# Turning the attention's mixed values on VectorE in 32x32 squares instead of on TensorE

## The chip, the core and the metric

The kernel runs on one core of one Trainium2 chip. The metric is the time of one launch on the device in microseconds (us), as the median of several runs; each run executes the whole kernel once. Besides, one execution is recorded by the hardware profiler, and every duration of a single instruction comes from that one.

The core has five engines that work side by side, each on its own queue, in order. PE is TensorE's matrix multiplication and PEld its loading of weights, DVE is VectorE, ACT is ScalarE, POOL is GpSimd, SP only issues transfers. TensorE writes its results to PSUM, a memory of eight banks of 512 f32 columns on 128 partitions; VectorE and ScalarE fetch them from there into SBUF, the working memory.

## The reference

The input is x of shape (8, 512, 256) in f32: 8 batches of 512 tokens. Four layers follow on each other, each on the normed x and added to x: a scan layer, a mixture of experts, an attention, and the same mixture again.

```
x = x + scan(layernorm(x))          # silu(x Win), decaying state, y Wout
x = x + ffn(layernorm(x))           # 16 routed experts, 4 chosen per token, and a shared one
x = x + attention(layernorm(x))
x = x + ffn(layernorm(x))

# attention, H = 16 heads of DK = 16, T = 512 tokens, per batch
q, k, v = split(x @ Wqkv.T)
scores  = clip(q @ k.T * 0.25, -10, 10) + causal_mask
out     = softmax(scores) @ v       # (H, T, DK) -> (T, 256)
return out @ Wout.T
```

The change is in the attention alone, between the product with v and the product with Wout.

## The kernel before

**Stages.** There are four: the scan, the blocks of the routed experts, the attention, and the routed blocks again. `stretch` runs the scan and, later, the attention over the eight batches. In each of them the norm, the router and the shared expert of the mixture that follows are worked in beside: while batch b has its attention, the shared expert of batch b - 2 and the router of batch b - 1 and b - 2 run, and the norm and the projections to q, k and v of the batches ahead. Batches 0 and 1 have no shared expert beside them.

**What sets the order.** Each piece of work is a generator that yields the number of TensorE columns of its next step. `beside` takes the next step from the piece that is least far on, by share of its columns; `behind` puts pieces one after another; `timed` places steps at given shares of the way. What comes out is a program, and a scheduling layer then sets the order on each engine from the dependences and its own costs, apart from instructions that are kept in program order.

**Buffers.** A pool has a number of buffers per tag, which its tiles take in turn: a new tile waits until the one whose buffer it gets has been read for the last time. In SBUF these are "col" (6 buffers of 512 columns: es of the third bank, oT, sig, the router's larger tiles) and "kb4" (9 buffers of 1024 columns). In PSUM the attention has four single banks ("one": po, pto, pt, pq, pv, pg, pd, py, pl, pr) and two pairs ("pair": the scores ps).

**The attention of one batch** (`Attention.main`, from L1100). The 16 heads are four groups (o, w): o is the half of the 256 columns, w says which of two neighbouring heads, and a group holds four heads, j = 0 to 3, each on 32 partitions. For a group:

- `weights` (L1120, L1131, L1134, L1142): the scores of four heads, transposed (key tokens on the partitions), into ps; ScalarE takes their exponential into es; VectorE clips it, and the causal triangle with it.
- `mix` (L1155): v times the weights into po, 128 partitions x 512 tokens. The stationary operand of a head has 32 columns: its 16 values, a column of ones, and 15 that are not needed. So po has for head j, on partitions 32j to 32j + 15, the mixed values not yet divided; on partition 32j + 16 the sum of the weights, by which they are to be divided; then 15 rows of no use.
- `share` (L1168 to L1174): the division. [...] ScalarE copies po to SBUF (oT, L1168), TensorE turns it in four 128x128 transposes into pto (L1171), where tokens lie on the partitions and the sum of a head is beside its values; VectorE takes the reciprocals (rec, L1173) and multiplies (o, L1174).

When all four groups are done, `turned` (L400, L402; tiles pt_oa and xT_oa) turns o back by eight 128x128 transposes, and ScalarE and VectorE each copy one half to SBUF, since the next product needs the 256 columns on the partitions. Then `add_projection` (L457, L466; tile py_a) multiplies by Wout and adds to x.

`weights` of a group is written before `mix` of the group before it, and `share` after both; in batches 2 to 6 (`close`) the two are one step.

The names that appear below besides: pq_a, pv_a (L1065, L1083) the projections to q, k and v, with L1076 VectorE's part of k; pg_m, pd_m (L982, L1011) the shared expert, with sig_m and act_m on ScalarE and VectorE (L996 to L1002); pt_m, pl_m (L400, L595) the router's transposes and logits, whose turning (L606) is a transpose of VectorE; pick, sel (L657, L665) the router's choice; rstd_l (L435) the norm's power on GpSimd; xg (L723) the scatter of the rows to their experts by GpSimd.

Of the kernel before, what the change touches and what calls it, by code (L numbers as in the profile page):

```python
# [10 lines left out]
FP = mybir.dt.float32  # L11
# [4 lines left out]
P = 128  # L16
SQ = 32
QUAD = P // SQ
B, T, D = 8, 512, 256
NT = T // P  # L20
KD = D // P
# [3 lines left out]
H, DK = 16, 16  # L25
HG = 4
NO = H * DK // P
# [29 lines left out]
KB, COLS = 9, 6  # L57
# [19 lines left out]
def tile_hybrid_block(  # L77
# [22 lines left out]
    nc = tc.nc  # L100
# [3 lines left out]
    work = ctx.enter_context(tc.tile_pool(name="work", bufs=2))  # L104
    small = ctx.enter_context(tc.tile_pool(name="small", bufs=2))
# [3 lines left out]
    def bank(shape, name: str, kind: str = "one"):  # L109
        kind = instead.get(kind, kind)  # L110
        return stage[kind].tile(shape, FP, tag=kind, name=name)
# [54 lines left out]
    ident = const.tile([P, P], FP, name="ident")  # L166
# [119 lines left out]
    steps = const.tile([P, NJ], FP, name="steps")  # L286
# [101 lines left out]
    def turned(src, tag: str, into, copies, home=None, past=None):  # L388

        rows = src()  # L390
        if home is None:
            dst = work.tile([P, KD, T], FP, tag="kb4", name=f"xT_{tag}", bufs=KB)
        else:
            dst = home(f"xT_{tag}")
        into(dst)
        for k in range(KD):
            pt = bank([P, NT, P], f"pt_{tag}_{k}")
            for t in range(NT):
                with tc.issue_after(past[-1].ins) if past else nullcontext():
                    nc.tensor.transpose(pt[:, t, :], rows[:, t, k * P : (k + 1) * P], ident)  # L400
            flat = pt.rearrange("p t q -> p (t q)")
            copies[k](dst[:, k, :], flat)  # L402
            yield T // 2

    by_both = (nc.scalar.copy, nc.vector.tensor_copy)
# [40 lines left out]
    def kb4(name: str):  # L446
        return work.tile([P, NT, D], FP, tag="kb4", name=name, bufs=KB)
# [583 lines left out]
    def spot(kind: str, rows: int):  # L1031
        first, many, n = spots[kind]
        spots[kind][2] = (n + 1) % many
        at = first_expert * WEXP + (first + n) * NT * D
        return w_all[:, at : at + NT * D].rearrange("p (a b) -> p a b", a=rows)

    class Attention:
# [60 lines left out]
        def main(self, b: int, made):  # L1098
            q_sb, k_sb, v_sb = made
            tag = f"a{b}"  # L1100
            held = {}

            def weights(o: int, w: int, i: int, at):


                tiles, cols = BANKS[i]
                ps, es = [], []
                for two in range(2):
                    name = f"{tag}_{o}_{w}_{i}_{two}"
                    ps.append(bank([P, 2, T], f"ps_{name}", "pair"))  # L1110
                    if cols == T:
                        es.append(spot("es", 2))
                    else:
                        es.append(work.tile([P, 2, cols], FP, tag="col", name=f"es_{name}", bufs=COLS))
                col = 0
                for c in tiles:
                    n = T - c * P
                    for j in range(HG):
                        r = slice(32 * j, 32 * j + 32)
                        nc.tensor.matmul(  # L1120
                            ps[j // 2][:, j % 2, col : col + n],
                            lhsT=k_sb[w][r, o, c * P : (c + 1) * P],
                            rhs=q_sb[r, o, c * P : T],
                            start=True,
                            stop=True,
                        )
                        at[c, j] = es[j // 2][:, j % 2, col : col + n]
                    col += n
                mixed = len(tiles) * P
                for two in range(2):  # L1130
                    nc.scalar.activation(es[two], ps[two][:, :, 0:cols], AF.Exp, scale=ATT_SCALE)  # L1131
                    diagonal = es[two][:, :, 0:mixed]
                    limit = causal[:, 0 : len(tiles), :].rearrange("p c q -> p (c q)")
                    nc.vector.scalar_tensor_tensor(  # L1134
                        diagonal,
                        diagonal,
                        LOW,
                        limit.unsqueeze(1).to_broadcast([P, 2, mixed]),
                        ALU.max,
                        ALU.min,  # L1140
                    )
                    nc.vector.tensor_scalar(es[two][:, :, mixed:], es[two][:, :, mixed:], LOW, TOP, ALU.max, ALU.min)  # L1142
                return T + (len(tiles) - 1) * T

            order = [c for tiles, _ in BANKS for c in tiles]

            def mix(o: int, w: int, i: int, at):


                if i == 0:  # L1150
                    at["po"] = bank([P, T], f"po_{tag}_{o}_{w}")
                for c in BANKS[i][0]:
                    for j in range(HG):
                        h = 8 * o + 2 * j + w
                        nc.tensor.matmul(  # L1155
                            at["po"][32 * j : 32 * j + 32, c * P : T],
                            lhsT=v_sb[:, c, h * VC : h * VC + 32],
                            rhs=at[c, j],
                            start=(c == order[0]),
                            stop=(c == order[-1]),  # L1160
                            tile_position=(0, 32 * j),
                        )
                return len(BANKS[i][0]) * T

            def share(o: int, w: int, at):

                oT = work.tile([P, T], FP, tag="col", name=f"oT_{tag}_{o}_{w}", bufs=COLS)
                nc.scalar.copy(oT, at["po"])  # L1168
                pt = bank([P, NT, HG, 32], f"pto_{tag}_{o}_{w}")
                for t in range(NT):  # L1170
                    nc.tensor.transpose(pt[:, t].rearrange("p j c -> p (j c)"), oT[:, t * P : (t + 1) * P], ident)  # L1171
                rec = small.tile([P, NT, HG], FP, tag="rec", name=f"rec_{tag}_{o}_{w}")
                nc.vector.reciprocal(rec, pt[:, :, :, DK])  # L1173
                nc.vector.tensor_mul(  # L1174
                    held["o"].rearrange("p t (o j w c) -> p t o j w c", o=NO, j=HG, w=2)[:, :, o, :, w, :],
                    pt[:, :, :, 0:DK],
                    rec.unsqueeze(3).to_broadcast([P, NT, HG, DK]),
                )

            def steps():  # L1180
                held["o"] = kb4(f"o_{tag}")
                groups = [(o, w, {}) for o in range(NO) for w in range(2)]

                close = 1 < b < B - 1
                last = None
                for o, w, at in groups:
                    for i in range(len(BANKS)):


                        columns = weights(o, w, i, at)  # L1190
                        if last is not None and not close:
                            yield columns
                            columns = 0
                        if last is not None:
                            columns += mix(*last[0:2], i, last[2])
                        yield columns
                    if last is not None:
                        share(*last)
                        yield T // 2
                    last = o, w, at  # L1200
                for i in range(len(BANKS)):
                    yield mix(*last[0:2], i, last[2])
                share(*last)
                yield T // 2
                yield from turned(lambda: held["o"], f"o{tag}", lambda oT: held.update(oT=oT), by_both)
                yield from add_projection(b, lambda c: held["oT"][:, c, :], wo_sb, KD, tag)

            each = 2 * NT * T + T // 2
            return Piece(2 * NO * each + KD * T // 2 + NT * KD * D, steps())


    ready, unturned = {}, {}
# [336 lines left out]
```

## Time and profile before

| what | us |
|---|---|
| median of 3 runs | 1742.05 |
| the runs | 1734.45, 1742.82, 1742.05 |
| the profiled execution | 1735.83 |
| its span, first to last instruction | 1734.1 |
| TensorE busy | 1648.4 (95%) |
| VectorE busy | 1110.7 (64%) |
| ScalarE busy | 788.7 (45%) |
| GpSimd busy | 773.0 (45%) |
| mean TensorE clock granted, share of full | 0.985 |

The attention goes from about 744 us (first projection) to about 1243 us (last product with Wout); from there to 1301 us the shared experts of batches 6 and 7 and the last router follow, then the routed blocks.

A row of a group of instructions reads: line, engine, operation, tiles written and read, shape, count; then the busy time in us and the mean ns of one; then the idle time of the engine just before, and what ended it. A row of the waits reads: who waited, for whom, us in total, times, longest. A row of the timeline reads: start and length in us, engine, line, operation, count. Matrix multiplications in f32 are two passes each in the trace, transposes one; they overlap in TensorE's pipeline, so the length of one is more than the time by which it delays the next.

### The profile page before, as it was taken

The numbers are of one execution on the slowest core, as the hardware profiler recorded it, in microseconds if no ns is written. First come the engines' busy times: TensorE is split into PE (matmuls) and PEld (weight loads), VectorE is DVE, ScalarE is ACT, GpSimd is POOL, SyncE is SP. The second block draws the span as 40 slices with busy tenths as digits, with TensorE's granted clock in tenths as the row PEclk, the third lists the DMA queues.
The fourth block names the chain that finished last, engine by engine and source line by source line (L and its number), as shares of the span: only waits on it lengthen the run. The fifth ranks groups of instructions, "written<-read, shape, count | busy, mean of one in ns | idle before, by whom it ended". The sixth has DMA issues, their size and how long they took to land. (4 is left out here: it accounts for less than half of the span.)

```text
span 1734.1 us, 32869 instructions
## 1 busy us (share of the span) xinstructions
PE 1648.4 (95%) x10640; PEld 1225.8 (71%) x10640; DVE 1110.7 (64%) x3463; ACT 788.7 (45%) x1724; POOL 773.0 (45%) x675
## 2 busy tenths in 40 slices
PE   6899998999999999999999999999998999998993
PEld 3566655589999999944445545544558999998992
DVE  7888877545556655566776676676754755565562
ACT  3223232155555555555544454364315555554551
POOL 3356556435555555530042332332543555555563
PEclk8999999999999999999999999999999999999997
DMA  4454423445555665531011212122544555566666
GB/s 160 147 179 151 148 93 121 153 95 95 96 95 104 105 101 95 106 62 38 25 65 50 77 51 72 55 73 84 192 138 89 96 96 97 111 138 124 122 120 166
DMA packets 149277, 181.37 MB, mean 105 GB/s; under 512 B 16144, under 2 KB 135984, under 8 KB 149104
## 3 DMA queue, kind: packets, MB, share of 16 engines
q0 software_dynamic: 54720, 82.57, 25.6%
q1 hardware_dynamic: 92576, 92.71, 17.9%
q10 hardware_dynamic: 1808, 3.93, 0.6%
q8 instruction: 89, 1.46, 0.4%
q14 instruction: 84, 0.69, 0.1%
HBM read 81.62 MB, written 97.53 MB: 103 GB/s over the span
## 5 line engine op out<-in xcount | busy, mean ns | idle before, releaser
L930 POOL DMA_INDIRECT part<-rows x272 | 425.9, 1566 | 341.5 <-ACT rows L929 236.7
L723 POOL DMA_INDIRECT xg<-sorted_m,slots_m x256 | 258.3, 1009 | 267.6 <-ACT slots_m L720 91.9
L893 PEld LDWEIGHTS ph<-rows,gate 128*128 128x128 f32 x2160 | 282.0, 191 | 16.1 <-ACT rows L883 1.9
L893 PE MATMUL ph<-rows,gate 128*128 128x128 f32 x2160 | 285.5, 275 | 0.6 <-ACT rows L883 0.6
L893 PE MATMUL ph<-rows,up 128*128 128x128 f32 x2160 | 285.3, 275 | 0.0
L921 PE MATMUL pyr<-w_all,rows 128*128 x1088 | 279.8, 380 | 0.4 <-DVE rstd_l L431 0.4
L893 PEld LDWEIGHTS ph<-rows,up 128*128 128x128 f32 x2160 | 262.9, 192 | 0.0
L901 ACT ACTIVATE rows<-ph 128x256 f32<-128x256 f32 x272 | 104.2, 383 | 328.5 <-PE ph L893 328.5
L902 DVE TENSOR_TENSOR rows<-ph,rows 128x256 f32<-128x256 f32 x272 | 115.2, 424 | 190.4 <-ACT rows L901 189.4
L921 PEld LDWEIGHTS pyr<-w_all,rows 128*128 128x128 f32 x1088 | 185.5, 190 | 14.9 <-ACT rows L929 0.8
L875 ACT COPY gate<-w_all 128x512 f32 x270 | 168.8, 626 | 14.2 <-PE ph L893 2.4
L1131 ACT ACTIVATE w_all<-ps_a 128x1024 f32<-128x1024 f32 x128 | 124.4, 1021 | 68.8 <-PE ps_a L1120 63.7
L875 DVE COPY up<-w_all 128x512 f32 x270 | 118.1, 437 | 30.3 <-PE ph L893 17.5
L929 ACT ACTIVATE rows<-pyr,gain 128x256 f32<-128x256 f32 x272 | 128.4, 472 | 14.3 <-PE pyr L921 12.2
L906 DVE SCALAR_TENSOR_TENSOR gain<-rows,expert_b 128x4 f32<-128x4 f32 x272 | 61.2, 225 | 107.9 <-ACT rows L929 82.4
L1120 PE MATMUL ps_a<-w_all 32*128 32x384 f32 (+3 forms) x1024 | 120.0, 468 | 8.0 <-ACT w_all L1131 6.3
L982 PE MATMUL pg_m<-xT_m,su_sb 128*128 128x512 f32 x256 | 123.4, 604 | 0.0
L982 PE MATMUL pg_m<-xT_m,sg_sb 128*128 128x512 f32 x256 | 122.3, 599 | 0.0
L903 DVE TENSOR_TENSOR rows<-ph,rows 128x256 f32<-128x256 f32 x272 | 115.0, 423 | 8.4
L1011 PE MATMUL pd_m<-sd_sb,act_m 128*128 128x256 f32 x512 | 120.0, 382 | 0.0
L1011 PEld LDWEIGHTS pd_m<-sd_sb,act_m 128*128 128x128 f32 x512 | 95.4, 190 | 22.0 <-issue 5.7
L882 PE MATMUL pt<-ident,rows 128*128 128x128 f32 x544 | 103.7, 273 | 6.2 <-DMA rows<-xg 4.8
(228 smaller groups left out, 2176.7 us busy)
## 6 DMA issues: line engine op xcount, KB each, us to landing
rows<-xg SPq DMA_DIRECT2D x272, 136.0 KB, 2.5
part<-x SPq DMA_DIRECT2D x16, 512.0 KB, 2.9
part<-ys_m SPq DMA_DIRECT2D x14, 512.0 KB, 3.1
w_all<-in_L_ffn_gate_w_dram SPq DMA_DIRECT2D x24, 256.0 KB, 5.4
w_all<-in_L_ffn_up_w_dram SPq DMA_DIRECT2D x24, 256.0 KB, 5.4
w_all<-in_L_ffn_down_w_dram SPq DMA_DIRECT2D x24, 256.0 KB, 5.8
sum<-part POOLq DMA_DIRECT2D x10, 512.0 KB, 4.1
xg<-zeros SPq DMA_DIRECT2D x34, 136.0 KB, 1.8
```

What stands on the lines that cost most here:

```text
L723: nc.gpsimd.indirect_dma_start(out=xg[i], out_offset=bass.IndirectOffsetOnAxis(ap=slots[:, at : at + 1], axis=0), in_=rows[:, t, :], in_of ...
L875: copy(here, w_all[:, bass.ds(held[n][0] + half * KD * F, KD * F)])
L893: nc.tensor.matmul(ph[:, s, f * P : (f + 1) * P], lhsT=both[s][:, k * F + f * P : k * F + (f + 1) * P], rhs=rows[:, ROW + k * P : ROW + (k ...
L902: nc.vector.tensor_mul(act, ph[:, 0, :], act)
L903: nc.vector.tensor_mul(act, ph[:, 1, :], act)
L921: nc.tensor.matmul(py, lhsT=act[:, f * P : (f + 1) * P], rhs=w_all[:, bass.ds(w + 2 * KD * F + f * D, D)], start=(f == 0), stop=(f == KF - 1),
L929: nc.scalar.mul(rows[:, 0:D], py, gain[:, TK : TK + 1])
L930: nc.gpsimd.indirect_dma_start(out=parts[i][n % 2], out_offset=bass.IndirectOffsetOnAxis(ap=rows[:, D + 2 * TK : D + 2 * TK + 1].bitcast(U ...
L982: made = nc.tensor.matmul(dst, lhsT=w[:, k, f * P : (f + 1) * P], rhs=xnT[:, k, :], start=(k == 0), stop=(k == KD - 1),)
L1011: nc.tensor.matmul(py[:, j, :], lhsT=acts[n][:, f, t * P : (t + 1) * P], rhs=shared[n][3][:, f, :], start=(n == 0 and f == 0), stop=(n == ...
L1120: nc.tensor.matmul(ps[j // 2][:, j % 2, col : col + n], lhsT=k_sb[w][r, o, c * P : (c + 1) * P], rhs=q_sb[r, o, c * P : T], start=True, st ...
L1131: nc.scalar.activation(es[two], ps[two][:, :, 0:cols], AF.Exp, scale=ATT_SCALE)
```

## The change

Instead of copying po and turning it on TensorE, VectorE's transpose reads po from PSUM and turns each square of 32 x 32 by itself, into the tile tr: square (j, q) of po, head j and tokens 32q to 32q + 31, stays in its place and is turned within it. So on partition 32j + s there is, in square q, token 32q + s of head j: 16 values and, in column 16 (DK), its sum. One reciprocal for each partition and square, and a multiplication, divide. The group w = 0 does so in place, in columns 0 to 15 of each square; the group w = 1 writes its divided values beside them, in columns 16 to 31 of the tile of w = 0 (`both`). A second transpose of VectorE then turns the squares back, into half o of oT; the squares' rows are now 32j + 16w + c, which is the order of the 256 columns of the product with Wout. oT is read there directly.

The copies by ScalarE, the four transposes of each group, the eight of `turned`, and its two copies go; and with them their steps in the generator (the steps of `share` count no columns now, and the piece's total is smaller by as much).

```diff
             def share(o: int, w: int, at):
 
-                oT = work.tile([P, T], FP, tag="col", name=f"oT_{tag}_{o}_{w}", bufs=COLS)
-                nc.scalar.copy(oT, at["po"])
-                pt = bank([P, NT, HG, 32], f"pto_{tag}_{o}_{w}")
-                for t in range(NT):
-                    nc.tensor.transpose(pt[:, t].rearrange("p j c -> p (j c)"), oT[:, t * P : (t + 1) * P], ident)
-                rec = small.tile([P, NT, HG], FP, tag="rec", name=f"rec_{tag}_{o}_{w}")
-                nc.vector.reciprocal(rec, pt[:, :, :, DK])
+                tr = work.tile([P, T // SQ, SQ], FP, tag="col", name=f"tr_{tag}_{o}_{w}", bufs=COLS)
+                nc.vector.transpose(tr.rearrange("p q c -> p (q c)"), at["po"])
+                rec = small.tile([P, T // SQ], FP, tag="rec", name=f"rec_{tag}_{o}_{w}")
+                nc.vector.reciprocal(rec, tr[:, :, DK])
+                both = held.setdefault(o, tr)
                 nc.vector.tensor_mul(
-                    held["o"].rearrange("p t (o j w c) -> p t o j w c", o=NO, j=HG, w=2)[:, :, o, :, w, :],
-                    pt[:, :, :, 0:DK],
-                    rec.unsqueeze(3).to_broadcast([P, NT, HG, DK]),
+                    both[:, :, w * DK : (w + 1) * DK],
+                    tr[:, :, 0:DK],
+                    rec.unsqueeze(2).to_broadcast([P, T // SQ, DK]),
                 )
+                if w == 1:
+                    nc.vector.transpose(held["oT"][:, o, :], both.rearrange("p q c -> p (q c)"))
 
             def steps():
-                held["o"] = kb4(f"o_{tag}")
+                held["oT"] = work.tile([P, NO, T], FP, tag="kb4", name=f"oT_{tag}", bufs=KB)
...
                     if last is not None:
                         share(*last)
-                        yield T // 2
+                        yield 0
...
                 share(*last)
-                yield T // 2
-                yield from turned(lambda: held["o"], f"o{tag}", lambda oT: held.update(oT=oT), by_both)
+                yield 0
                 yield from add_projection(b, lambda c: held["oT"][:, c, :], wo_sb, KD, tag)
 
-            each = 2 * NT * T + T // 2
-            return Piece(2 * NO * each + KD * T // 2 + NT * KD * D, steps())
+            return Piece(2 * NO * 2 * NT * T + NT * KD * D, steps())
```

In the kernel after, the first transpose has line L1168, the reciprocal L1170, the multiplication L1172 and the second transpose L1178; lines after that are lower by two than before.

## The prediction

> **What bounds the kernel now.** I read the busy totals first, then the stretches of the attention stage, its groups of instructions, TensorE's waits, and the timeline of one batch's end.
>
> ```profile
> PE 1648.4 (95%) x10640; PEld 1225.8 (71%) x10640; DVE 1110.7 (64%) x3463; ACT 788.7 (45%) x1724; POOL 773.0 (45%) x675
> ```
> ```profile
> 803.00:851.00 48.00, 46.39 (x362) 22.01 (x361) 38.33 (x125) 27.73 (x40) 3.23 (x4) 1.00 0.11 34
> ...
> 1045.00:1110.00 65.00, 64.23 (x408) 32.03 (x404) 44.79 (x132) 31.99 (x54) 18.25 (x18) 1.00 0.16 55
> ...
> 1175.00:1244.00 69.00, 64.37 (x453) 33.48 (x452) 50.82 (x175) 28.69 (x51) 23.75 (x26) 1.00 0.41 135
> ```
>
> The second fence is busy time by stretch: start:end, length, then PE, PEld, DVE, ACT, POOL. The three rows are about batch 1, a middle batch and batch 7 of the attention. TensorE has nearly no idle time in any; VectorE stands at 38.33/48 = 80%, 69% and 74%. A microsecond of TensorE's queue that goes is therefore a microsecond of the span, unless TensorE then waits. Who makes it wait now (first to last microsecond of the attention proper, 744 to 1244):
>
> ```profile
> PE ps_a L1120 <- ACT w_all L1131: 6.3, 12, 1.0
> PE pto_a L1171 <- DVE w_all L1076: 2.5, 4, 0.8
> PE pto_a L1171 <- ACT oT_a L1168: 1.1, 1, 1.1
> PE pt_oa L400 <- DVE o_a L1174: 1.0, 1, 1.0
> ```
>
> Three of the four lines, 4.6 us, stand before the very transposes that the change deletes. The groups concerned, and the one stream transpose that the kernel already has:
>
> ```profile
> L1171 PE MATMUL pto_a<-ident,oT_a 128*128 128x128 f32 x128 | 19.8, 277 | 3.7 <-DVE w_all L1076 2.5 <-ACT oT_a L1168 1.1
> L400 PE MATMUL pt_oa<-ident,o_a 128*128 128x128 f32 x64 | 9.9, 278 | 1.0 <-DVE o_a L1174 1.0
> L1168 ACT COPY oT_a<-po_a 128x512 f32<-128x512 f32 x32 | 19.0, 592 | 30.4 <-PE po_a L1155 28.0 <-DVE row_m L678 2.4
> L1174 DVE TENSOR_TENSOR o_a<-pto_a,rec_a 128x256 f32<-128x256 f32 x32 | 13.5, 422 | 0.7
> L1173 DVE RECIPROCAL rec_a<-pto_a 128x16 f32<-128x16 f32 x32 | 8.1, 252 | 12.8 <-PE pto_a L1171 12.8
> L402 DVE COPY xT_oa<-pt_oa 128x512 f32<-128x512 f32 x8 | 5.5, 692 | 9.5 <-PE pt_oa L400 9.5
> L606 DVE STREAM_TRANSPOSE logit_m<-pl_m 128x128 f32<-128x128 f32 x16 | 5.0, 312 | 18.0 <-PE pl_m L595 17.9
> ```
>
> The mean of 277 ns is the length of one transpose, not what it costs the queue. That is read from successive starts at the end of batch 0:
>
> ```profile
> 798.91 0.50 PEld L1171 LDWEIGHTS pto_a<-ident,oT_a 128*128 128x128 f32 x4
> ...
> 799.38 0.47 PEld L400 LDWEIGHTS pt_oa<-ident,o_a 128*128 128x128 f32 x4
> ...
> 799.82 0.73 PEld L1083 LDWEIGHTS pv_a<-w_att,xT_l 128*128 128x128 f32 x4
> ```
>
> Four transposes take 0.47 and 0.44 us, on average 0.455.
>
> [...]
>
> **The change, part by part.**
> *Removed from TensorE:* per batch 4 blocks for pto and 2 for pt_oa, of four each; in 8 batches 48 x 0.455 = 21.8 us. With them go the 4.6 us of waits in front: 26.4 us at most.
> *Removed from ScalarE:* per batch 4 x 0.592 + 0.585 (its half of xT_oa) = 2.95 us, 24 us in all. ScalarE is at 45 to 60% in these stretches; the saving counts only where the exponentials (L1131) hold TensorE, the 6.3 us above. I take nothing and keep 6 us for the good end.
> *VectorE.* Removed per batch: 4 x (0.252 + 0.422) + 0.692 = 3.39 us. Added: 4 transposes of 128x512 from PSUM, 2 from SBUF, 4 reciprocals and 4 multiplications, now from SBUF. PSUM rows of 256 and 512 columns (0.422, 0.692) give 1.05 ns per column, so 0.312 + 384 x 1.05 ns = 0.71 us. From SBUF I take 0.70; the lower end is 0.437, which a 128x512 SBUF copy takes (L875), the upper for both 1.25 = four times 0.312. Reciprocal 0.25 and multiplication 0.41 (SBUF rows of that size, L690) as now. Sum 4 x (0.71 + 0.25 + 0.41) + 2 x 0.70 = 6.9 us: 3.5 more per batch, 28 us in all. A middle batch goes from 44.8/65 to 48.3/62 = 78%, batch 1 to some 41.8/45 = 93%. It is beside TensorE, but the queue is in order.
> *The new wait* is at each batch's end. Built, the program puts behind the last mixing matmul one py_a, two pd_m pairs, one py_a, a pd_m, and then the py_a whose weights are the second half of oT. Each is two passes of 0.215 us (16 passes of py_a take 3.81 us with the tail), so that is 7 x 0.43 = 3.0 us of cover. The chain on VectorE: the drain of po 0.3, transpose 0.71, reciprocal 0.25, multiplication 0.41, transpose 0.70, with the router's pick and sum (0.41 + 0.58) queued between: some 3.3 us. The stall is 0.3 us in middle batches, about 0.5 in batches 0, 1 and 7, whose cover is other work. If the scheduler's neighbours are late, 1.5 us. Behind the waiting py_a stand the next batch's scores, and so ScalarE.
> *PSUM.* po's bank is now freed by VectorE (0.71 us, in order behind the clips L1134 and L1142), not by ScalarE. Where VectorE is behind, as in the first group of a middle batch, where pto waited 0.8 us for L1076, the next po or pg waits. 4 + 2 of 34 banks per batch are no longer asked for, which works the other way. I put 0.4 us per batch on it.
> *SBUF.* The "col" tile of w = 0 now lives until the group w = 1 is turned back, one of six gone for a quarter of a batch; a "kb4" tile per batch is saved. Priced under the rivals.
> *POOL:* four xg scatters stand ahead of the power of rstd_l (L435) in batches 2 to 5; they take 1.27 us each from start to start, the xn that waits stands over ten us later, so nothing. No DMA is added; SP's order is the same.
>
> Sum: 26.4 - 8 x (0.4 + 0.4) = 20.0, less 1 for batch 1 at 93%: **19 us saved**; ends 8 and 32.
>
> **The rivals.** *A, as above.*
> *B, it saves more:* fewer PSUM banks and a freer ScalarE also end the 6.3 us of ps_a waits, and py_a never waits: 26.4 + 6 = 32 us. For it: three of four waits sat there. Against: VectorE's queue.
> *C, VectorE's lateness takes back most:* at 1.25 us per transpose its time per batch grows by another 6 x 0.54 = 3.3 us, and chain and bank waits cost 1.5 to 2.5 us per batch: 26.4 - 16 = 10 us or less saved; about nothing at 3 us per batch.
> *D, slower:* the held col tile. ScalarE's exponentials of the third bank (es_a) and sig_m come from the same six buffers; if each of the 32 groups has one that waits for VectorE's turn back, TensorE stops behind it. It decides above 26.4/32 = 0.8 us per group; at 1.2 us it is 12 us slower. Against it: some 22 col tiles per batch, so the sixth after is mostly past the release.
> *E, the saving is not in the span* because the scatters of batch 7 set the end of the stage: they end at 1291.6 us and TensorE's work before the routed blocks at 1301, so 9 us are free. Excluded unless the scatters slip.
>
> **How the numbers follow.** The profiled execution took 1735.8 us (span 1734.1); the runs have 1734.5, 1742.1 and 1742.8, so it is 6 us below their median. Half of the runs lie at either level; I start from 1738. A: 1738 - 19 = **1719** (1708 to 1732), chance 0.62. B: 1706, 0.14. C: 1728 to 1738, 0.17. D: 1750, 0.07. The range, 1703 to 1736, leaves out D and the ends. A measurement of this kernel can tell about 0.5%, some 9 us: faster (below 1733.3) 0.83, same 0.10, slower 0.07.
>
> **What would show it.** Right: no pto or pt_oa rows; TensorE's gaps before py_a under 5 us in all; the two transpose groups near 0.71 and 0.70 us; VectorE 27 us busier, ScalarE 24 less; the attention 20 us shorter, all other stages as they were. Wrong: transposes over 1 us, PE waits on L1168 or L1178 above 10 us, or es_a and sig_m waiting for VectorE.

## The result and the profile after

The kernel after takes 1729.24 us (median of 7 runs, 1726.29 to 1733.52), the kernel before 1738.88 us (7 runs): a ratio of 0.9943, 95% interval 0.9926 to 0.9961. That is faster by about 10 us, where the prediction's sum was 19 us. Two further sets of runs gave 0.9946 [0.9927, 0.9965] and 0.9934 [0.9908, 0.9959]. The profiled execution took 1730.08 us (span 1728.4).

The engines' totals, as the page has them:

```profile
PE 1638.1 (95%) x10448; PEld 1210.7 (70%) x10448; DVE 1131.6 (65%) x3503; ACT 767.9 (44%) x1684; POOL 772.8 (45%) x675
```

192 matrix multiplications are gone, VectorE is 20.9 us busier, ScalarE 20.8 less busy. The groups that the change brings, from the groups of instructions:

```profile
L1168 DVE STREAM_TRANSPOSE tr_a<-po_a 128x512 f32<-128x512 f32 x32 | 22.7, 710 | 24.6 <-PE po_a L1155 24.6
L1178 DVE STREAM_TRANSPOSE oT_a<-tr_a 128x512 f32<-128x512 f32 x16 | 11.2, 697 | 0.3
L1172 DVE TENSOR_TENSOR tr_a<-tr_a,rec_a 128x256 f32<-128x256 f32 x32 | 13.3, 417 | 0.2
L1170 DVE RECIPROCAL rec_a<-tr_a 128x16 f32<-128x16 f32 x32 | 7.8, 245 | 0.0
```

The durations are those of the prediction: 0.710 and 0.697 us for the transposes (0.71 and 0.70 taken). So VectorE's prices are not where the 9 us went. The waits of TensorE in the attention (744 to 1244 us) say more:

```profile
PE ps_a L1120 <- ACT w_all L1131: 6.7, 15, 1.0
PE pt_l L400 <- DVE tr_a L1168: 2.6, 1, 2.6
PE po_a L1155 <- DVE tr_a L1168: 2.0, 4, 0.5
PE pr_m L673 <- DVE sel_m L665: 2.0, 1, 2.0
```

The waits in front of pto and pt_oa are gone. Two single waits have come, of 2.6 us (pt_l, in batch 1) and 2.0 us (pr_m, the router's product, in batch 7), and a small one in four of the middle batches. The timeline shows the two:

```profile
843.79 0.71 DVE L1168 STREAM_TRANSPOSE tr_a<-po_a 128x512 f32<-128x512 f32 x1
844.55 0.66 PE L400 MATMUL pt_l<-ident,xn 128*128 128x128 f32 x4 [2.57 <-DVE tr_a L1168]
1221.08 0.43 PE L673 MATMUL pr_m<-sel_m,tri 128*128 128x64 f32 x2 [1.99 <-DVE sel_m L665]
```

pt_l wants the bank of a po that the transpose at 843.79 has to read first, and that transpose stands on VectorE behind the router's choice (L641 to L654) and two clips. In batch 7 sel stands behind a transpose (L1168, from 1219.33) and more clips; whether that transpose is why TensorE waits is taken up under e4.

The last thing to see is in the busy time by stretch, in the third column from the right, the granted clock of TensorE (start:end, length, then PE, PEld, DVE, ACT, POOL). The first two rows are about batch 1 and a middle batch, the others lie in batch 7:

```profile
803.00:852.00 49.00, 44.17 (x339) 19.51 (x338) 41.08 (x131) 26.07 (x36) 3.23 (x4) 1.00 0.11 33
1045.00:1110.00 65.00, 64.42 (x405) 31.00 (x404) 49.27 (x153) 29.28 (x49) 20.08 (x20) 1.00 0.17 60
...
1184.89:1191.72 6.83, 6.83 (x33) 1.89 (x29) 6.62 (x24) 3.39 (x7) 0.00 (x0) 0.50 0.14 41
1191.72:1222.44 30.72, 27.22 (x230) 10.77 (x228) 25.47 (x86) 14.72 (x25) 16.81 (x16) 1.00 0.50 167
1222.44:1225.85 3.41, 3.41 (x7) 1.17 (x4) 1.72 (x7) 0.93 (x4) 0.00 (x0) 0.50 0.64 178
```

In two stretches, 6.83 and 3.41 us long, the clock is 0.50. The second begins 1.4 us after the wait for sel ends. TensorE counts as fully busy in them (6.83 of 6.83), so neither busy time nor waits show the loss: 7 instructions take the 3.41 us. The profile before had no such stretch in the attention.

Batches, from the last py_a of one to that of the next (starts in the timeline; batch 0 from the first pq_a), in us:

| | 0 | 1 | 2 | 3 | 4 | 5 | 6 | 7 | sum |
|---|---|---|---|---|---|---|---|---|---|
| before | 60.2 | 48.0 | 69.2 | 67.9 | 67.6 | 67.8 | 66.0 | 51.6 | 498.3 |
| after | 58.0 | 49.3 | 65.0 | 65.2 | 65.2 | 65.2 | 63.5 | 55.9 | 487.3 |
| saved | 2.2 | -1.3 | 4.2 | 2.7 | 2.4 | 2.6 | 2.5 | -4.3 | 11.0 |

Six batches gain 2.2 to 4.2 us, where the prediction's terms give 2.5 for one; batches 1 and 7 lose. With the 5.1 us that the two stretches at half clock cost at most (half of 10.24), batch 7 would be 50.8 us.

### The profile page after: what moved, and what is told of

It reads as the page before. It is cut to its first block, busy times and chain, and to the rows that moved or that the text cites. A ratio compares the mean times of both kernels' runs of the same rounds, so it can differ in the third digit from the quotient of the medians.

```text
span 1728.4 us, 32460 instructions
## 1 busy us (share of the span) xinstructions
PE 1638.1 (95%) x10448; PEld 1210.7 (70%) x10448; DVE 1131.6 (65%) x3503; ACT 767.9 (44%) x1684; POOL 772.8 (45%) x675
```

## The experiments

**Two theories.** *1:* the gain in TensorE's queue came through, less two single waits (batches 1 and 7); the rest went to TensorE's clock, which is halved after a wait. *2:* VectorE's lateness, spread over the batches and reached through po's banks, took it; the clock only accompanies it.

Each run lists its granted clock, so the clock's share can be estimated for runs without a profile too: time x (1 - clock), called the clock loss below; what is left of the time is the rest. For the profile of after this gives 37.9 us, which is half of what its stretches at 0.50 last. Two limits go with it. It counts also the stretches of the first 355 us, 12 us of loss in each profile of the two kernels, and the last one, where TensorE has no work: 24 to 25 us long in the two profiles of before, 26 to 28 in the three of after, so about 1 us of a difference between the two may be no loss. And it is an upper estimate: a stretch of 6.83 us in batch 7 of before (under e1) made that batch 1.6 us longer, not 3.4.

The runs in a table (medians; "clock loss" and "rest" are means over the runs; batches from the profile; runs of one kernel in several sets are joined in the first two rows, whose times are means). The runs of before come from three chips, and on each the rest is 1708.6 to 1709.3 us. The means of five to eight runs have standard errors of 0.6 to 1.9 us, so 2 us between two of these kernels are hardly clear of the scatter.

| kernel | us | ratio to before, 95% | clock loss | rest | batches 0, 1, 7 |
|---|---|---|---|---|---|
| before (85 runs) | 1739.3 | 1 | 30.4 | 1708.9 | 60.2, 48.0, 51.6 |
| after (23 runs) | 1728.9 | see above | 35.9 | 1693.0 | 58.0, 49.3, 55.9 |
| e3 old in batch 7 | 1725.1 | 0.9921 [0.9893, 0.9950] | 31.9 | 1692.9 | 59.3, 50.9, 53.2 |
| e4 po by ScalarE | 1727.6 | 0.9938 [0.9915, 0.9961] | 35.8 | 1692.0 | 59.8, 47.7, 55.6 |
| e5 fill | 1727.1 | 0.9933 [0.9908, 0.9958] | 31.1 | 1695.6 | 57.3, 50.8, 58.3 |
| e6 before, fill | 1739.1 | 0.9996 [0.9981, 1.0012] | 26.9 | 1710.8 | 59.5, 48.0, 51.7 |
| e7 sel first | 1725.1 | 0.9912 [0.9882, 0.9942] | 34.1 | 1689.7 | 59.4, 50.9, 53.0 |
| e8 all three | 1723.7 | 0.9908 [0.9881, 0.9936] | 31.0 | 1692.0 | 57.3, 47.7, 56.1 |
| e14 fill for sel | 1727.3 | 0.9924 [0.9899, 0.9949] | 33.5 | 1693.9 | 62.1, 50.8, 55.2 |
| e15 product later | 1723.0 | 0.9897 [0.9864, 0.9929] | 33.0 | 1689.6 | 59.7, 50.8, 53.5 |
| e16 all | 1720.8 | 0.9887 [0.9857, 0.9916] | 30.7 | 1690.2 | 57.3, 47.7, 54.6 |

The batches of before and after are those of the first profiles. The second profile of before has 61.4, 48.0 and 53.2 us, the second and third of after 62.6, 50.9, 55.9 and 58.0, 49.3, 56.0.

**e1 and e2, the two kernels once more, for their clocks.**

> The kernel before, unchanged, for the granted clock of several of its executions. In its one profile 1.7 us are lost between 500 and 1700 us to stretches in which TensorE's clock is halved (one stretch, at 1306.5), in the profile of the kernel after 11.95 us (six, two of them in batch 7). Theory 1, the change makes such stretches more frequent: the clocks of the runs here are 0.983 to 0.986 (those of after were 0.977 to 0.983, mean 0.980), so 5 to 8 us of the missing gain are clock. Theory 2, the stretches fall by luck and VectorE's queue took the gain: the clocks here scatter around 0.980 too, and the profile of this run has some of the stretches between 1000 and 1700.

> The kernel after, unchanged, once more. Theory 1: the halved stretches near 1184.9 and 1222.4 (the end of batch 7) come again in this profile, though the 3.41 us grid on which the clock is set lies elsewhere, since the waits in front of them (1.0 us for the exponential, 2.0 us for the router's sel) are in the program's order: at least one of the two. Theory 2: they need not come again, but batch 7 then stays longer than before's 51.6 all the same. Time 1727 to 1732, ratio 0.993 to 0.996.

Over all sets the clock loss is 30.4 us before (standard error 0.4) and 35.9 us after (0.7): 5.6 us more, 95% about 4.0 to 7.1. The rest is 16.0 us less (14.8 to 17.1). Theory 1 holds in that, though before's clocks were lower than I expected (0.979 to 0.986, mean 0.9826). The second profile of before has a stretch of 6.83 us in batch 7 too, after a wait of 1.0 us for the exponential, and one of 3.41 us in batch 0:

```profile
1202.50:1209.33 6.83, 6.83 (x35) 1.85 (x30) 6.35 (x24) 3.26 (x6) 0.00 (x0) 0.50 0.14 38
```

So these two can come without the change, as theory 2 had it; whether the change makes them more frequent, two profiles of before can't tell. (The expectation speaks of six stretches in after; they are five, at 1184.9, 1222.4, 1294.1, 1543.3 and 1580.8.) The second profile of after has both stretches of batch 7 again, at 1192.2 and 1229.7, and one more behind the wait of pt_l in batch 1:

```profile
847.43:850.84 3.41, 0.83 (x8) 0.42 (x4) 3.31 (x21) 0.00 (x0) 0.00 (x0) 1.00 0.00 0
850.84:854.26 3.42, 3.42 (x21) 1.78 (x20) 1.17 (x3) 0.00 (x0) 0.00 (x0) 0.50 0.01 2
```

In 3.41 us TensorE was busy for 0.83, and the next 3.41 us are at 0.50. In the first profile the same wait lay across the edge of two such windows (1.58 and 0.99 us idle), and no stretch followed.

**e3, batch 7 as before.** `share` of the kernel before for `b == B - 1`.

```diff
+                if b == B - 1:
+                    oT = work.tile([P, T], FP, tag="col", name=f"oT_{tag}_{o}_{w}", bufs=COLS)
+                    nc.scalar.copy(oT, at["po"])
...
+                    return
```

> The kernel after, but batch 7 divides and turns as in the kernel before (ScalarE's copy, TensorE's 24 transposes), which is about 2.7 us more for TensorE. Theory 1: with the transposes back in batch 7, the wait for sel and the halved stretches there go, so batch 7 takes 51.6 instead of 55.9 us and the whole 1724 to 1727 us, a ratio of 0.991 to 0.993, at a mean clock 0.002 to 0.003 higher than after's. Theory 2 (VectorE's lateness is spread over all batches): batch 7 is worth at most 2 us and the ratio stays at 0.993 to 0.996.

With 24 transposes more the kernel is 4.8 us faster than after beside it (means; 95% about 0.6 to 9). The wait for sel is gone, and its stretch; the one after the exponential stays (at 1188.2), so batch 7 has 53.2 us and not 51.6, as in the second profile of before. The clock loss is smaller (31.9 against 35.9), and the rest did not grow by the transposes' 2.7 us, since the 2.0 us of the wait went.

**e4, po's bank freed by ScalarE.**

```diff
+                raw = work.tile([P, T], FP, tag="col", name=f"raw_{tag}_{o}_{w}", bufs=COLS)
+                nc.scalar.copy(raw, at["po"])
-                nc.vector.transpose(tr.rearrange("p q c -> p (q c)"), at["po"])
+                nc.vector.transpose(tr.rearrange("p q c -> p (q c)"), raw)
```

> The kernel after, with po copied to a col tile by ScalarE (0.59 us, as in the kernel before), and VectorE's first transpose reading that tile: po's PSUM bank no longer waits for VectorE's queue, VectorE's work is the same. Theory 2, bank waits: the waits for the transpose (po 2.0 us, pt_l 2.6 us) and of the weights go, 4 to 8 us faster than after, ratio 0.989 to 0.991. Theory 1: the waits go, but they are worth at most their 4.6 us; the time falls by 2 to 5 us, less what 32 more copies on ScalarE delay the exponentials (0 to 4 us): ratio 0.991 to 0.994.

All waits for tr_a are gone. Batch 1 takes 47.7 instead of 49.3 us and has no stretch at half clock, the middle batches 65.0 instead of 65.2. So the bank is the cause in batch 1, and worth 0.2 us in a middle batch, of 0.4 us put on it. The whole is 1.8 us faster than after beside it, give or take 2.9, so not clear of the scatter: the wait for sel grew to 2.8 us.

```profile
1220.93 0.57 DVE L665 TENSOR_REDUCE sel_m<-pick_m 128x64 f32<-128x256 f32 x1
1221.42 0.70 DVE L1170 STREAM_TRANSPOSE tr_a<-raw_a 128x512 f32<-128x512 f32 x1
1221.56 0.43 PE L673 MATMUL pr_m<-sel_m,tri 128*128 128x64 f32 x2 [2.84 <-DVE sel_m L665]
```

Here sel stands in front of the transpose, and TensorE waits longer than in after. Counted from the last py_a of batch 6, sel is done after 43.6 us in e4, 43.7 in after and 43.5 in the second profile of before, each with the same stretch of 6.83 us earlier in the batch. So the change hardly delayed sel. What it changed is TensorE: without its transposes it is ready for the router's product 41.8 us into the batch in after, and 40.8 us in e4, where the product stands eight mixing products earlier in its queue. In before it comes to it at 44.3 us and waits for nothing. TensorE became early; VectorE's transposes did not make sel late.

**e5 and e6, idle transposes in after and in before.**

```diff
+                many = {(0, 1): 4, (0, 2): 8, (B - 1, 2): 8}.get((b, i), 0) if o == w == 0 else 0
+                if many:
+                    spare = bank([P, T], f"spare_{tag}_{i}")
+                    with tc.issue_after(held["ps"].ins):
+                        for n in range(many):
+                            nc.tensor.transpose(spare[:, 0:P], ident, ident)
```

> The kernel after with 20 more transposes of the constant ident by TensorE, whose result nobody reads: 4 and 8 of them stand in front of the scores of the second and third bank in the first group of batch 0, 8 in front of those of the third bank in the first group of batch 7. There TensorE waits for the exponential (0.5, 0.4, 0.9 and 1.0 us) and, in the profiles so far, the clock is halved right after. The 20 cost 2.2 us of TensorE's queue, in the waits' time. Theory 1 (the clock): the stretch of 6.8 us near 1185 is gone and that near 765 too, so the kernel with more work is 3 to 6 us faster than after, 1723 to 1726 us, ratio 0.990 to 0.993, mean clock at least 0.982. Theory 2 (the clock is a symptom, or falls by luck): no change or up to 2 us slower, 1729 to 1731 us, clock 0.978 to 0.980.

> The same 20 transposes in the kernel before. Its second profile has the same stretches near 765 and 1202, its first has not. Theory 1: the clock rises from 0.9825 to 0.984 or more and the time falls by 2 to 4 us, to 1735 to 1737 us; if so, these two stretches are not of the change's making, and what the change adds to the clock's loss are those after its own waits (sel in batch 7, pt_l in batch 1). Theory 2: within 1 us of before.

In batch 0 the stretch is absent in both. The place in after without and with the transposes; first two rows of e2:

```profile
762.10:765.51 3.41, 1.77 (x18) 0.97 (x20) 1.96 (x5) 2.86 (x5) 0.00 (x0) 1.00 0.76 256
765.51:775.75 10.24, 10.24 (x40) 2.60 (x40) 4.76 (x12) 3.96 (x5) 0.00 (x0) 0.50 0.06 19
```

and one row of e5:

```profile
761.90:768.70 6.80, 6.20 (x48) 2.87 (x48) 4.97 (x13) 5.62 (x8) 0.00 (x0) 1.00 0.44 151
```

Batch 0 takes 57.3 us, against 58.0, 62.6 and (e13, below) 58.0 in the three profiles of after. In batch 7 they do fill the wait that they were meant for: 0.2 us are left of 1.0, and no stretch follows. But the batch got longer (58.3 us), since TensorE then waits 2.1 us for a later exponential. That one stands on ScalarE behind slots_m, which waits for VectorE:

```profile
1185.61 0.70 PE L1126 MATMUL ps_a<-w_all 32*128 32x256 f32 x4 [0.21 <-ACT w_all L1137]
1190.42 0.29 ACT L720 CAST slots_m<-choices_wm 128x2 uint32<-128x2 f32 x2 [1.40 <-DVE choices_wm L696]
1191.68 1.14 PE L1126 MATMUL ps_a<-w_all 32*128 32x128 f32 x12 [2.08 <-ACT w_all L1137]
```

In after TensorE runs through that place at half clock and does not wait there. In e5 a stretch of 3.41 us follows this wait, and one of 6.83 us the wait for sel. As a whole e5 gained 1 to 2 us and e6 nothing: the clock loss fell (by 4.8 and by 2.7 to 3.5 us), and the rest grew by about the 2.2 us of the transposes. More TensorE work for no time, then, but not the 3 to 6 us that I expected.

**e7, sel earlier on VectorE; e8, all three together.** In e7 pick and sel get a higher priority in the scheduling layer, and the transpose of the third group is queued behind sel:

```diff
+                late = b == B - 1 and summed.get((1, B - 2))
+                with tc.issue_after(late.ins) if late else nullcontext():
+                    nc.vector.transpose(tr.rearrange("p q c -> p (q c)"), at["po"])
```

> The kernel after, but in batch 7 the router's pick and sum (sel) are put ahead of two clips and of the transpose of the third group on VectorE's queue, some 1.25 us earlier. The wait of the router's product for sel is 2.0 us in after. Theory 1: it becomes 0.7 us, [...] so the stretch of 3.4 us near 1222 (1.7 us lost) goes as well: 3 us faster than after, 1726 us, ratio 0.992 to 0.993. Theory 2, only the wait itself counts, and VectorE's work behind it is as late as before: at most 1.3 us, ratio 0.994.

> The kernel after with the three together: po copied by ScalarE, sel first in batch 7, the 20 idle transposes. If the waits and the clock are independent terms, they add: 1.5 us of waits (batch 1 and the small ones) with 1.7 us of clock after them in part of the runs, 3 us for sel, 3 to 6 us for the transposes: 1719 to 1723 us, ratio 0.988 to 0.991, clock 0.983 or more. If they overlap or VectorE's lateness only moves on to the next wait, 1724 to 1727 us.

e7 is some 4 us faster than after (theory 1 said 3), but not as it said: sel is done 1.1 us earlier (42.6 us into the batch), but the scheduling layer put the router's product ten mixing products earlier too, and it still waited, 2.3 us. That wait was cut by a window's edge (1.42 and 0.90 us), and no stretch followed; batch 7 took 53.0 us. In e8 the wait was 3.0 us, the stretch was back and the wait of 2.1 us that e5 has in batch 7 came too: 1723.7 us, just outside what independent terms gave.

**e9 to e12, the waits for sel and VectorE's load,** ran on a chip where the kernel before itself took 1770.6 us: its stages with much transfer were longer, the clock loss 44 us.

> The kernel after with its wait for sel in batch 7 left as it is, but filled: when pick is there, about 0.5 us into the wait, TensorE turns it 14 times into a part of the bank of pr that nobody reads (14 x 0.109 = 1.5 us), and then waits for sel as before. VectorE's queue is the same, and the router's product can start no earlier. Theory 1, the clock follows from how little TensorE does in a stretch of 3.41 us: with 0.5 us of idle time in place of 2.0 the stretch at half clock near 1222 to 1230 is gone, batch 7 is 1.7 us shorter (54.2 instead of 55.9 us), the whole 1 to 2 us faster than after. Theory 2, it follows from something else (VectorE's lateness, heat, luck): the stretch comes as in both profiles of after, and batch 7 takes 55.9 us or a little more.

> The kernel after, but the step of the router in batch 7 that issues its product with sel comes at 0.84 of the batch instead of 0.76 (and the steps behind it at 0.86 to 1.0 instead of 0.79 to 1.0), so that TensorE has some 3.5 us of mixing and of the shared expert in the place where it waited 2.0 us for sel. VectorE is as late as in after. Theory 1: wait and stretch go, 2.0 + 1.7 = 3.7 us, batch 7 52.2 us, the whole 1725 to 1726 us, ratio 0.992. Theory 2 (what VectorE is late with reaches TensorE in any case): the wait is found again at po, py or pt of the same batch, and at most 1 us is won.

> The kernel after without the division: reciprocals and multiplications are left out, and so is the second half of the turned values, which takes 0.66 us from each of the 32 groups on VectorE, 21 us in all, as much as the change has added to it. It is to show what VectorE's load costs. Theory 2 (VectorE's lateness took most of the missing gain): 6 to 10 us faster than after, the middle batches at 63.5 to 64.3 instead of 65.2 us. Theory 1 (places in the queue and the clock, not the load): the middle batches gain 0.2 to 0.4 us each (the chain at their end is 0.66 us shorter), the waits for sel and in front of pt_l shrink by 0.7 us each: 2 to 4 us in all.

> A version for use: the kernel after with po copied by ScalarE (batch 1), sel ahead of the third group's transpose, the router's product later in batch 7, and the 12 idle transposes of batch 0 alone. From the parts: 1.5 us and 1.7 us of clock in part of the runs (batch 1), 3.7 us (sel), 0.7 us and up to 1.7 us of clock (batch 0): 1721 to 1723 us, ratio 0.989 to 0.991, clock 0.982 to 0.984, batches 57.3, 47.7, 64.8, 65.0, 65.0, 65.0, 63.6 and 52 us.

Their batch 7 can't be read beside the others, since it has waits that no earlier profile has: in e11 and e12 one of 2.5 us for an exponential, in e9 and e10 TensorE's instructions themselves came late, 2.0 and 1.6 us (the line is of e9):

```profile
PE ps_a L1127 <- issue: 2.0, 2, 1.5
```

Ratios to before: e9 0.9910 [0.9887, 0.9933], e10 0.9925 [0.9903, 0.9947], e12 0.9896 [0.9874, 0.9919]. The middle batches are not touched by that. For e11 (no reciprocal, no multiplication; its router sees other values and its routed blocks take 427 us instead of 396 to 403 in the other three, so that its total of 1779.1 us tells nothing) they are the answer. A middle batch of it:

```profile
1000.00:1064.40 64.40, 64.36 (x405) 31.24 (x404) 47.93 (x146) 29.29 (x49) 20.28 (x21) 1.00 0.21 69
```

and one of after:

```profile
983.00:1048.20 65.20, 64.61 (x406) 31.17 (x405) 49.18 (x153) 29.29 (x50) 20.22 (x20) 1.00 0.20 67
```

2.6 us less of VectorE are worth 0.8 us in a middle batch, between what the two theories said; TensorE is then busy for 64.36 of 64.40 us. So VectorE's lateness in the middle batches costs about 0.8 us, which is in the sum what the prediction put on it (0.4 + 0.4). In batch 1, without the wait of pt_l, it is worth more: 46.1 us against 49.3, if half of a stretch of 6.83 us is set aside, which stands there behind a wait of 1.8 us for an exponential.

**e13 to e16, the same questions beside after on one chip.**

> The kernel after beside the next three, on one chip. In the runs of the four kernels before these, batch 7 held waits that no earlier profile has (TensorE's instructions came late twice, 1.5 us, and the stages with much transfer took some 10 us longer in the kernel before as well), so what they say of batch 7 is not settled. Theory 1: batch 7 with the wait for sel (2.0 us) and two stretches at half clock, 55.9 us, ratio 0.993 to 0.996.

> The wait for sel filled with 14 idle transposes, as in the run of this kernel before. Theory 1: no stretch at half clock after sel (near 1222 to 1230), batch 7 at 54.2 us if the stretch after the exponential (near 1185) is there, 1 to 2 us faster than after. Theory 2: the stretch is there, batch 7 at 55.9 us.

> The router's product issued later in batch 7, as in the run of this kernel before. Theory 1: wait and stretch gone, 3.7 us, batch 7 at 52.2 us, ratio to before 0.992. Theory 2: at most 1 us, the wait is found elsewhere in the batch.

> The version for use once more, beside after on the same chip: 5 to 8 us faster than after, ratio to before 0.989 to 0.991, batch 7 at 52 us, batch 1 at 47.7 us.

e13 has the two stretches of batch 7 for the third time (56.0 us). e14 gives TensorE useless work inside the wait for sel, and places that step of the router at 0.785 of the batch instead of 0.76:

```diff
+        pr = bank([P, 4 if idle else 2, NT, E], f"pr_{tag}")
+        if idle:
...
+                for n in range(14):
+                    nc.tensor.transpose(spare, some_rows, ident)
```

Its stretches around the wait:

```profile
1217.70:1224.54 6.84, 6.43 (x66) 2.24 (x58) 6.46 (x34) 3.03 (x4) 2.97 (x3) 1.00 0.63 207
1224.54:1227.95 3.41, 1.81 (x16) 1.51 (x15) 2.68 (x9) 0.00 (x0) 0.00 (x0) 1.00 1.06 362
1227.95:1231.37 3.42, 3.42 (x19) 1.47 (x20) 2.27 (x10) 0.93 (x4) 0.00 (x0) 1.00 0.69 211
```

and the wait in its timeline:

```profile
1226.44 1.75 PE L677 MATMUL pr_m<-ident,pick_m 128*128 128x128 f32 x14 [1.59 <-DVE pick_m L657]
1228.03 0.33 PE L680 MATMUL pr_m<-sel_m,tri 128*128 128x64 f32 x2
```

From the last mixing product to the router's product it is now 3.2 us instead of 2.0 (pick came later than I had assumed), of which 1.59 idle, and the clock stays at 1.00. Batch 7 is 0.8 us shorter all the same: 1.7 us of clock won, about 1 us of wait lost. The runs are no faster than those of e13 (1727.3 and 1727.5 us), where theory 1 said 1 to 2 us: the loss of clock fell by 2.3 us and the rest rose by 2.1 us, both hardly clear of their scatter, and as the profile says. So in this profile the clock follows what TensorE does in its window, not VectorE's lateness. e15 moves only the waiting instruction:

```diff
-                        timed(some(r.rest, PICKS), *spread(0.57, 0.67, PICKS - 1), 0.76),
+                        timed(some(r.rest, PICKS), *spread(0.57, 0.67, PICKS - 1), 0.84 if layer.mixture else 0.76),
```

(and the steps behind it in the same way). Its waits:

```profile
PE pt_m L400 <- DVE sorted_m L440: 2.0, 1, 2.0
PE pr_m L673 <- DVE sel_m L665: 1.0, 1, 1.0
```

The wait for sel falls to 1.0 us, 1.2 us of it come back at pt_m (0.8 in after), and no stretch follows either: batch 7 at 53.5 us, the kernel 4.4 us faster than after beside it (by the means 5.0 us, 95% about 1.5 to 8.5). e16, with po by ScalarE, sel first, the product later and the idle transposes in batch 0 alone, is the best: 1720.8 us, 6.7 us below after on that chip and 1.1% below before. Its batch 7 has 54.6 us and not the 52 expected. Of the wait for sel 0.3 us are left, but the next one has grown, and a stretch of 3.41 us at half clock follows it:

```profile
PE pt_m L401 <- DVE sorted_m L441: 2.3, 1, 2.3
```

## Why the prediction was wrong, and where it was right

In short: TensorE's queue became shorter by what was forecast, but in batches 1 and 7 it then waited at one place each, and it ran more often at half clock. The sum had no term for the clock and looked for the waits at other places.

**Right, with sizes.** *TensorE is the bound:* the 48 blocks and their waits did come out of the span. Batches 0 and 3 to 6 save 2.2 to 2.7 us each; the prediction's own terms give 26.4/8 - 0.8 = 2.5. *The prices* of VectorE's instructions. That a transpose takes as many ns more per column as VectorE's other reads from PSUM (1.05) was the author's assumption; after has 310 ns for the router's 128x128 (L606) and 710 for 128x512, 1.04 ns per column. *VectorE's lateness in a middle batch,* 0.8 us (e11), but with some luck: of its two terms of 0.4 us the bank measured 0.2 (e4), and the chain at the batch's end next to nothing, since no py_a waits for the change by more than 0.2 us. *Rivals B and D:* the waits for the exponential stay (6.7 against 6.3 us), and the exponential into es_a stops nowhere for the held tile. One of the signs of being wrong did come: ScalarE's sig_m waits 6.3 us for VectorE, once, in batch 7 of all three profiles of after and of neither of before. TensorE's waits behind the shared expert's chain come to 0.2 us, so it cost little. *The other signs:* VectorE is 20.9 us busier and not 27, ScalarE 20.8 less and not 24. In the first profiles the attention is 11 us shorter and not 20, and the rest of the launch is 5.3 us longer, up to 5.1 of it by stretches at half clock between 1290 and 1600 us.

**The first step that failed: "A microsecond of TensorE's queue that goes is therefore a microsecond of the span, unless TensorE then waits".** It takes TensorE's speed as fixed. The profile before had the clock at 1.00 in all three rows that I showed, and I carried that over. After it is not so: by the estimate above 5.6 us (4.0 to 7.1) of the gain go to halved clock, at most. This term stood at nothing, and no rival had it; it is the larger part of the miss. Where the change's own waits bring it: behind the wait for sel in the three profiles of after and in e4, e5 and e8; not in e3, where the wait is gone, in e7, where a window's edge cuts it, nor in e14 and e15, where it is filled or shorter; behind the wait of pt_l in one of three profiles of after and in e3, e5, e7, e14 and e15, which have that wait, and in none of four kernels without it (e4, e8, e12, e16; a fifth, e11, has its stretch in batch 1 behind another wait). That is 2.3 us at most, averaged over the three profiles of after. What after loses more at other places (behind the exponentials of batches 0 and 7, at the start of the routed blocks, and from 1540 to 1590 us) was not taken apart; those stretches come and go from profile to profile, before has some of them, and why after has more is open.

The reading in front of that step was too favourable as well: "nearly no idle time in any" fits batch 1 and the middle batch, but the third row, which is mostly batch 7, has 4.6 us idle in 69.

**The second: the PSUM term, "0.4 us per batch", and "less 1 for batch 1 at 93%".** An even price was put on a wait that falls on single places. In the middle batches it was 0.2 us (e4); in batch 1 it was one wait of 2.57 us. Batch 1 should have saved 1.5 us and lost 1.3: 2.8 us short. In batch 7 the "unless TensorE then waits" came true where it was not looked for: the new wait was sought at py_a, but TensorE, relieved of its transposes, came to the router's product 2.0 us before sel, which was hardly later than in before (e4). With the clock set aside the batch saved 0.8 instead of 2.5 us: 1.7 us short. Batch 2 saved 4.2 us, 1.7 more than worked out; why is open. 19 - 2.8 - 1.7 + 1.7 - 0.1 (the others) = 16.1 us by the profiles; the rest, over all runs, fell by 16.0. That the two agree so closely is partly chance, since half of a stretch is only the most that it can cost. Less 5.6 of clock it is 10.4, the difference of the means (1739.3 and 1728.9), as it must be: the rest is what the clock loss leaves of the time.

Rival C had the right result, 10 us, by the wrong cause (1.25 us per transpose).

## What to carry to other kernels

When work goes from the engine that bounds, ask not only which wait takes its place, but whether that engine is then idle for a microsecond or two at one place: in batch 7 of after, behind waits of 1.0 and 2.0 us, TensorE ran the next 6.8 and 3.4 us at a granted clock of 0.50, which shows as busy time. Take the granted clock of short stretches, and time x (1 - clock) of all runs, before explaining a difference under 1%. Look for places where the relieved engine now arrives before its input, on any chain and not only the changed one: in batch 7 it was the router's. And price the lateness of an in-order queue at the places where others wait for it: an average per batch was right for six batches and missed the two that mattered. Moving the one waiting instruction (e15) gained 4 to 5 us.

## What the runs showed of the hardware

**The clock.** In the profiles of before and after the stretches at 0.50 last 3.41 us or two or three times that (6.83, 10.24), apart from the last one, which the launch's end cuts. In each of the two profiles they lie on one grid of 3.41 us throughout, and this grid lies elsewhere in before than in after. So the same wait can be followed by a stretch in one execution and not in another: that of 2.6 us in front of pt_l was in the second profile of after (at 850.8), and was not in the first, where the grid's edge cut it into 1.58 and 0.99 us. At 0.50 TensorE is about half as fast: four passes of pg_m from 1222.45 on take 3.66 us in after, where four at 1.00 take 1.98 us (at 1197.56). How much idle time in one window of the grid brings a stretch in the next is not settled by these profiles: 1.99 us did (sel, three times of three), and 1.00 us where the rest of the window held scores of 32 rows and the router's products of 64 columns (after, batch 7, at 1181.5), while 1.01 us beside scores and two products of 512 columns (before, batch 7, at 1193.8), 1.59 us with 14 full transposes (e14) and 1.58 us beside four transposes and eight mixing products (after, batch 1, at 840.1) did not. A limit in idle time alone does not fit these.

**VectorE's busy time.** The four new groups sum to 55.0 us and the removed ones to 27.1, a difference of 27.9, but VectorE's busy total rose by 20.9. In the timeline the instruction behind a transpose of 0.70 us starts 0.63 us after it (1210.32 to 1210.95): durations overlap by some 0.07 us, and a queue is shorter than the sum of its rows. Over all of VectorE's instructions the sum of durations rose by 24.8 us, so overlap is 3.9 of the 7.0 us; the other 3.1 are that rows the change did not touch became shorter, the clips of es_a by 1.8 us.
